# FFN rows turned by VectorE block transposes and DMAs instead of TensorE, with quotients on GpSimd and ScalarE and rounding in place

## The chip, the cores and the metric

The kernel runs on one core of a Trainium2 chip. The metric is the device time of one execution in microseconds (us); lower is better. A core has five engines that run side by side, each with an instruction stream of its own that is carried out in order: PE (TensorE, the matmuls, with PEld for its weight loads), DVE (VectorE), ACT (ScalarE), POOL (GpSimd) and SP (SyncE, which here issues DMAs). They wait for one another through semaphores.

## The reference

Sixteen sequences x of 256 rows and 256 channels pass through one block. Cut to what matters:

```python
# attention of 16 heads, projected, RMS-normalised, scaled and shifted by the condition
x1 = rwkv(adaln_attention(x))      # below
def rwkv(x):                       # x: (B, T, C); a shifted copy xx of x is mixed in
    k, v, r = xk @ Wk.T, xv @ Wv.T, xr @ Wr.T     # xk = x*mix_k + xx*(1-mix_k), and so on
    # scan over T: out_t = (a + exp(u + k_t) * v_t) / (b + exp(u + k_t))
    #              a, b = a*ew + exp(k_t)*v_t, b*ew + exp(k_t)
    return (sigmoid(r) * out) @ Wo.T
x = x + x1
x2 = quaternion_rotation(x)        # one 256 x 256 linear map
def fp4_linear(x, w):              # both operands rounded to FP4 in blocks of 16, with scales
    return einsum('bsk,nk->bsn', fp4_quant_dequant(x), fp4_quant_dequant(w))
gate, y = fp4_linear(x2, w_gate), fp4_linear(x2, w_up)         # 704 columns each
out = x + fp4_linear(silu(gate) * y, w_down)
```

## The kernel before, in words

Each of the 16 sequences (b from 0 to 15) goes through stages, each a Python generator that yields after a few instructions. The names in brackets are those of the stages in the order string.

- `ask` (a): load x, turn it (L599), project to q, k and v.
- `attend` (t): scores on PE (L650), exponentials on ACT (L659), values on PE (L671). `values` turns the sums into `u` on DVE (L681). `divide` then takes reciprocals (L688), multiplies (L690) and turns the rows back into `oT` (L696), all on DVE.
- `leave` (l): output projection, RMS norm and modulation, giving `xm` and the shifted `xx`.
- `mix` (m): the difference `d` on POOL (L759), three mixed inputs `mx` on DVE (L764), three projections on PE (L565), exponentials `ek` (L781) and `er` (L795) on ACT, two scans on DVE (L774). Then the quotient: `den` and `num` on DVE (L799, L803), `den` times 1 + er (L806), one reciprocal (L808), and the product `yT` on POOL (L811).
- `rotate` (r): output projection (the L565 with `wt_ao`), the residual `x1T` (L821), rotation (L826), a turn by 32 x 32 blocks (L830), rounding to FP4 (`quant`) and a turn back (L834).
- `hidden` (h for rows 0 to 127, i for rows 128 to 255): eight matmuls for gate and up (L847), tanh on ACT (L858), two products on DVE (L860, L864) and `quant` on the 704 columns.
- `quant`: block maxima, scale, reciprocal and a product on DVE (L486 to L490), absolute values on ACT (L492), two rounding steps on DVE (L494, L495), and the product with the scales on POOL (L498). It reads `src` and writes a tile `v` of its own.
- `turn_h` (d, e): the six 128-column pieces of a rounded row tile are transposed on PE (L541, by `turn_half`) and copied from PSUM to `hT` on ACT (L544, L549). `hT` has one buffer.
- `down` (f): twelve matmuls with `downT` and `hT` (L881), the sum with `x1T` and a turn on DVE (L886, L887), and four stores on SP (L892).

The weights go through similar stages at the start (W, V, with copies from PSUM on ACT at L533 and L544). Each matmul on f32 data shows as two records in the profile, each transpose as one.

The order of the instructions is not left to a scheduler. The string `ORDER` names one stage per word, and each word advances that stage by one yield; so it fixes the order on PE, ACT, DVE, POOL and SP:

```python
    with tc.manual_schedule(engines={E_.PE, E_.Activation, E_.DVE, E_.Pool, E_.SP}):
        for step in ORDER.split():
            if step not in made:
                made[step] = stages[step]()
            next(made[step])
```

The end of the string, from late in the last sequence's rotation, shows what runs there: `hf` and `if` are the two halves of its hidden stage, `fe` and `ff` the last two down projections.

```
rf fd he he he fd fd rf he if he ee if if he if if if if ee he he if ee hf if ee if if hf hf hf hf hf if if if
hf hf hf de hf de de hf de hf hf fe hf ef fe fe ef ef df ef fe fe df df df ff ff ff ff ff
```

After the main part a check of the reciprocals can branch to a slow exact path (`exact`, L923); with these inputs it is not taken.

Of the kernel before, what the change touches and what calls it, by code (L numbers as in the profile page):

```python
# [27 lines left out]
L L L L W1 L Q Q L a0 a0 W1 K L W1 W5 L K K Q Q W1 R L a0 W1 Q Q a0 a0 L a0 K R W5 K W5 R W1 a0 W1 A K a0 K t0 L  # L28
W0 A L W5 W5 t0 M A t0 W5 A R W5 a1 t0 M O t0 a1 t0 R W0 a1 W3 a2 W0 V0 t0 W3 O W2 t0 W3 W3 a1 t0 W0 R a1 t0 M
t0 R W0 a1 a1 t1 R A V0 W3 M a1 t1 t1 A W0 W3 t1 t0 W0 t1 V1 M R R t1 W3 t0 M W2 t1 a2 t0 t0 W2 A t0 t1 t1 a3 T  # L30
A t0 V0 V0 t0 V0 a2 t1 t1 W2 V1 a2 a2 a2 a3 W2 t1 t1 l0 t1 W4 t1 a2 T l0 V0 a2 t1 t1 t1 W4 l0 l0 l0 V0 a3 l0 t2
l0 m0 m0 V1 m0 t2 W4 W4 m0 W4 a3 a3 t2 m0 m0 a3 m0 m0 m0 t2 t2 t2 m0 l1 l1 m0 t2 m0 l1 l1 m0 m0 m0 m0 m0 t2 t2
l1 t2 V0 a3 t2 t2 a4 l1 l1 V0 t2 a3 r0 W2 W4 m1 m1 V1 r0 t2 t2 m1 m1 m1 V1 W2 m1 t3 m1 W4 t2 t2 r0 m1 t3 t2 r0
r0 a4 m1 t3 t3 t3 t3 r0 l2 l2 l2 m1 m1 m1 m1 m1 m1 m1 m1 l2 t3 t3 t3 r0 l2 a4 t3 l2 t3 t3 a4 a4 t3 l2 r1 r1 a4
a4 r0 r0 t3 r1 m2 t3 V1 V1 a5 a5 a4 m2 i0 t4 t3 r1 r1 t4 r1 m2 i0 i0 t3 t3 i0 i0 m2 m2 t4 i0 m2 m2 i0 i0 a6 i0
i0 i0 i0 i0 l3 l3 l3 l3 m2 m2 m2 m2 m2 t4 t4 t4 a5 a5 a5 a5 a5 t4 t5 r1 r1 m2 m2 m2 m2 h0 a5 h0 h0 t4 l3 r1 h0
t5 m2 i0 l3 h0 h0 h0 h0 h0 t5 l3 r2 t4 h0 h0 h0 t4 i1 i1 r2 h1 h1 h0 i1 i1 h1 t4 t4 i1 r2 r2 t4 h0 t4 h1 h1 t4
h1 h1 h1 r2 r2 a6 V1 t5 h1 t5 m3 t4 V1 h1 h1 r2 a6 a6 i1 t4 t4 r2 m3 i1 r2 h1 i1 i1 i1 i1 a7 a6 a6 t5 i1 h1 h1
m3 m3 i1 m3 m3 a6 a6 t5 t5 t5 t5 i2 i1 e0 t5 t5 i2 e0 t6 i2 i2 t6 t6 i2 m3 m3 m3 m3 i2 i2 i2 e0 t6 e0 i2 i2 i2
m3 m3 m3 d0 d0 t6 t6 h2 l4 m3 m3 m3 h2 l4 l4 h2 t5 m3 i2 h2 h2 h2 h2 l4 l4 t5 i2 h2 h2 h2 h2 i2 r3 t5 d0 r3 l4  # L40
t6 l4 t6 a7 t5 d0 h2 m4 m4 m4 m4 t5 a8 h2 t6 t6 m4 m4 a7 m4 t5 m4 r3 t6 m4 m4 t6 r3 a7 m4 t6 t6 m4 a7 m4 m4 m4
t6 a7 a7 l5 t7 r3 a7 m4 m4 t7 r3 r3 t6 l5 l5 r3 f0 t6 t7 l5 t6 t7 f0 f0 f0 t7 t7 d1 r4 r4 d1 d1 t7 d1 h2 l5 l5
l5 m5 a8 r4 t7 t7 f0 e1 r4 a8 r3 e1 r4 r4 m5 m5 i3 i3 i3 i3 a8 m5 t7 m5 i3 m5 m5 r4 r4 e1 e1 t7 t7 a8 a8 i3 i3
i3 i3 i3 i3 l6 t8 t8 t8 i3 i3 f1 t8 l6 l6 f1 h3 m5 t8 i3 l6 h3 m5 h3 h3 h3 l6 t8 l6 h3 h3 a8 a9 h3 t7 l6 t7 m5
m5 m5 h3 h3 h3 h3 a8 f1 m5 m5 m5 t8 m5 t8 m6 t7 t7 f1 m5 r4 t7 h3 t8 i4 i4 i4 i4 t8 t8 r5 r5 i4 i4 i4 e2 i4 a9
a9 e2 i4 m6 a9 i4 r5 i4 t8 r5 i4 t8 t8 t8 a9 a9 a9 e2 e2 t8 t7 h3 t9 r5 a9 r5 r5 t8 d2 d2 d2 d2 i4 l7 l7 m6 t9
m6 m6 l7 l7 i4 f2 m6 m6 m6 t9 h4 f2 m6 l7 h4 f1 h4 m6 t8 l7 h4 h4 l7 m6 m6 m6 m6 t9 m6 l8 m6 r5 l8 r5 h4 t9 l8
m6 l8 f2 f2 f2 h4 h4 i5 h4 h4 h4 i5 i5 i5 i5 r6 r6 l8 t9 h4 h4 l8 e3 t9 t9 e3 h4 aa aa l8 t9 i5 i5 aa t9 t9 m7
m7 i5 i5 d3 t9 t9 aa i5 d3 e3 i5 r6 r6 r6 e3 ab d3 d3 t9 m7 i5 i5 i5 aa aa aa h5 aa t9 h5 h5 h5 h5 h5 h5 h5 h5
h5 ta t9 m7 m7 r6 r6 m8 m7 h5 h5 m7 m8 f3 t9 f3 h5 ta f3 f3 ta f3 ta m7 r6 r6 ta h5 m8 ta d4 d4 e4 e4 m7 m7 m7  # L50
m7 m7 m7 m7 m7 m7 ta ta ta m8 m8 m8 ta i6 i6 i6 i6 i6 i6 i6 r7 m8 ta ta i6 i6 i6 h6 h6 r7 ab ta ac h6 m8 h6 h6
ta ta h6 i6 m8 m8 ab t9 h6 h6 h6 h6 ab ab ab i6 h6 ta i6 tb tb d4 ta h6 e4 m8 ta m8 h6 l9 d4 e4 ab r7 l9 i6 m8
f4 ab l9 m8 tb l9 h6 l9 m8 m8 m8 r7 f4 f4 r8 r7 e5 l9 l9 d5 tb r7 e5 d5 f4 r8 e5 m9 d5 m9 m9 m9 d5 m9 m9 la e5
r7 ac la r7 r7 la m9 m9 m9 la tb tb m9 m9 m9 m9 m9 m9 m9 m9 ac ac ac ac f5 f5 r8 r8 r8 la la la r8 r8 tb tb tb
r8 f5 f5 i7 i7 r8 ma tb tb tb i7 i7 i7 i7 i7 i7 i7 i7 i7 tc tc r9 r9 e6 h7 tc e6 i7 i7 ad ma ma ma tb tb h7 ad
h7 h7 tb r9 r9 f4 ac tc ac h7 r9 tc r9 i7 h7 h7 h7 h7 h7 tc h7 e6 e6 ma ma ma ma ma tb ma h7 tc tc tc tc ma ad
tb tb ma ma ma f5 h7 ad i8 i8 i8 i8 d6 i8 ad d6 h8 ad d6 d6 h7 ma ma h8 h8 h8 r9 ma h8 h8 h8 h8 i8 r9 h8 h8 h8
i8 i8 h8 r9 lb lb tc lb lb i8 i8 i8 f6 f6 f6 lb h8 h8 lb f6 e7 ra tc i8 e7 lb tc ra tc tc i8 f6 i9 i9 i9 i9 ra
mb mb i9 i9 i9 i9 ra i9 tc td ra d7 d7 ae tc ad i8 i9 i9 e7 td d7 tc ad mb mb ae d7 i9 e7 td mb mb h9 h9 h9 h9
td h9 h9 h9 af i9 ra lc ra ra td h9 h9 h9 h9 td lc lc lc td td i9 mb mb f7 mb mb h9 lc lc lc f7 f7 mb ra f7 mb  # L60
e8 ae mb ia td ia e8 mb ia ae mb h9 ia mc td mb mb ia ia ia ia ia f7 td ae ae d8 d8 ia ia ia h9 rb rb af mc ia
td td ae td td rb d8 d8 ae td te te ia mc mc ha rb rb td ha ha ha ha ha ha ha ha e8 mc ha ha td rb rb e8 te mc
mc mc te rb ha f8 mc mc mc mc ld te te mc ld rb mc ld f8 f8 mc mc mc te te te ld ib f8 ha d9 ib ib ib te te te
rc rc ib ib d9 ib ib ib ha f8 ld rc ld ld te te ib e9 hb af te e9 ib rc hb rc hb d9 ib hb rc te md md md af d9
hb e9 ib e9 ib te md md te C md rc af hb md af tf hb md hb f9 hb hb hb hb md md md md md md tf tf f9 f9 le le tf
tf f9 hb af rc rc ic ic le md f9 af le md md ic ic ic ic tf ic ic ic ic ic le rd le le ea tf rd ic me me da hb
ea ea ic ic rd da ea tf rd tf rd da me me me tf tf hc da me tf tf hc hc hc rd rd tf me hc me me me rd rd hc hc
tf hc hc hc hc hc tf tf tf fa fa me hc me me fa fa fa lf id lf id id me me lf lf eb eb C id lf id hc me lf lf db
id id id mf db hd id id id me hd db hd hd id hd re eb eb id re mf db hd hd fb hd hd hd hd fb dc re re id re hd
fb mf ec fb dc hd hd mf re ec ec mf mf re ec dc dc re mf mf mf mf fc ed re fc fc fc mf dd ed ie fc mf mf mf dd  # L70
mf mf mf ie ie ie ie ie ie ie ie ie ie ed ed fb rf ie C dd rf he he C ie dd ie he he rf rf rf fd rf he rf he fd
rf fd he he he fd fd rf he if he ee if if he if if if if ee he he if ee hf if ee if if hf hf hf hf hf if if if
hf hf hf de hf de de hf de hf hf fe hf ef fe fe ef ef df ef fe fe df df df ff ff ff ff ff
# [4 lines left out]
def kernel(  # L78
# [128 lines left out]
    def loads():  # L207
# [31 lines left out]
        load_w("av", a_v, "xr")  # L239
# [25 lines left out]
    gain = const.tile([P, E2, NB], F32, tag="gain", name="gain")  # L265
    uu = const.tile([P, E2], F32, tag="uu", name="uu")
# [42 lines left out]
    def turn_mask():  # L309
# [29 lines left out]
    def modulate():  # L339
# [5 lines left out]
        nc.vector.tensor_copy(wcT, pc[0:NC, :])  # L345
# [23 lines left out]
    def times():  # L369
        ew = const.tile([P, E2], F32, tag="ew", name="ew")  # L370
        nc.scalar.activation(ew, col("decay", 0, 2), AF.Exp, scale=1.0 / S)
        nc.scalar.activation(uu, col("first", 0, 2), AF.Exp, scale=1.0 / S)
        yield
        nc.vector.tensor_copy(ew_row, ew.unsqueeze(2).to_broadcast([P, E2, S]))
        yield
# [103 lines left out]
    def quant(src, n, tag, bufs, put=lambda dst: None):  # L479
        blk = lambda a: a.rearrange("p (b i) -> p b i", i=16)  # L480
        am = qp.tile([P, 44], F32, tag="am", name="am")[:, 0 : n // 16]
        rs = qp.tile([P, 44], F32, tag="rs", name="rs")[:, 0 : n // 16]
        v = qp.tile([P, 704], F32, tag="v", name="v")[:, 0:n]
        m = qp.tile([P, 704], BF16, tag="m", name="m")[:, 0:n]
        bc = lambda a: a.unsqueeze(2).to_broadcast([P, n // 16, 16])
        nc.vector.tensor_reduce(am, blk(src), AX.X, ALU.max, apply_absolute_value=True)  # L486
# [3 lines left out]
        nc.vector.scalar_tensor_tensor(blk(v), blk(src), -(1.0 - 2.0**-22), bc(rs), ALU.mult, ALU.mult)  # L490
# [17 lines left out]
    hT = wk.tile([P, FK, S], F32, tag="hT", name="hT")  # L508
    nc.gpsimd.memset(hT[FF % P : P, FK - 1, :], 0.0)
    nc.gpsimd.memset(downT[FF % P : P, FK - 1, :], 0.0)  # L510

    def in_weights(j):
        j *= 2 * P
        nt = min(2, (2 * FF - j) // P)
        n = nt * E
        raw = wk.tile([P, FF], F32, tag="h", name="raw", bufs=2)[:, 0:n]
        for jj in range(nt):
            lo, hi = j + jj * P, j + (jj + 1) * P
            for src, base in ((w_gate, 0), (w_up, FF)):
                a, b = max(lo, base), min(hi, base + FF)  # L520
                if a < b:
                    nc.sync.dma_start(out=raw[a - lo : b - lo, jj * E : (jj + 1) * E], in_=src[a - base : b - base, :])
        yield
        wq = yield from quant(raw, n, "hq", 4)
        pt = ps()
        for ct in range(E2):
            for jj in range(nt):
# [311 lines left out]
    def hidden(b, tt):  # L839
        xqT = xqs[b]  # L840
        for f in range(2):
# [20 lines left out]
            if f == 0:  # L862
                h = wk.tile([P, FF], F32, tag="h", name="h", bufs=2)
# [197 lines left out]
```

## Time and profile before

| | |
|---|---|
| median of 3 runs | 687.19 us (685.79 to 691.19) |
| profiled execution, its time | 686.15 us |
| its span, first to last instruction | 684.1 us |
| granted TensorE clock, mean | 0.994 |
| matmuls L847 (gate and up) | 512 records, 164.6 us busy |
| matmuls L881 (down) | 384 records, 90.2 us busy |
| transposes L541 | 204 records, 32.6 us busy (192 of hidden rows, 12 of weights) |
| copies into hT, ACT L544 and L549 | 15.2 + 12.0 + 8.4 us |
| product L498 with the scales, POOL, 704 columns | 1.40 us each, 34 of them |
| difference L759, POOL, 256 columns | 0.86 us each |

How to read it: "busy" is the time in which an engine has an instruction under way. A group's row gives line, engine, operation, what it writes and reads, shape and count, then busy time in us and the mean duration of one in ns, then the engine's idle time just before these instructions and what ended it. A PE record's duration includes the latency of the pipeline, so neighbouring matmuls overlap; their pace is the distance between their starts. A line of the timeline gives the start, the time from the first start to the last end of the merged instructions, and their number.

### The profile page before, as it was taken

How to read it: one execution, taken by the hardware profiler on the slowest of the kernel's cores; microseconds unless marked ns; L12 is line 12 of the kernel's file. 1: busy time of each engine (PE TensorE's matmuls, PEld its weight loads, DVE VectorE, ACT ScalarE, POOL GpSimd, SP SyncE). 2: the span in 40 equal slices, each digit the busy share in tenths (PEclk: the TensorE clock that was granted, in tenths of full speed). 3: DMA queues.
4: the chain of work that ended last, by engine and by line, in shares of the span. 5: the costliest groups of instructions: out<-in, count | busy, mean ns of one | idle time of the engine just before them, and what ended most of it. 6: DMA issues, size and time to landing. Idle time of an engine off the chain costs nothing. (4 is left out here: it accounts for less than half of the span.)

```text
span 684.1 us, 10332 instructions
## 1 busy us (share of the span) xinstructions
PE 661.7 (97%) x3880; PEld 464.2 (68%) x3880; DVE 587.8 (86%) x991; ACT 349.1 (51%) x765; POOL 142.7 (21%) x171
## 2 busy tenths in 40 slices
PE   7999999999999999999999999999999999898994
PEld 6657667656676666766667866767767676676663
DVE  6788797899996787888989888998899999999981
ACT  2777774655645645565435554455544556332230
POOL 4712220311203110122103110222112213111210
PEclk9999999999999999999999999999999999999997
DMA  6410000000001000020000100010000000001001
GB/s 173 116 53 17 1 16 17 1 16 0 1 17 32 1 3 15 0 47 1 16 17 0 32 16 2 0 32 1 17 0 17 1 16 1 16 1 31 13 4 36
DMA packets 39726, 13.61 MB, mean 20 GB/s; under 512 B 36068, under 2 KB 39284, under 8 KB 39668
## 3 DMA queue, kind: packets, MB, share of 16 engines
q1 hardware_dynamic: 39552, 12.85, 7.6%
q8 instruction: 32, 0.52, 0.3%
q14 instruction: 26, 0.21, 0.1%
q10 hardware_dynamic: 116, 0.02, 0.0%
HBM read 8.67 MB, written 4.19 MB: 19 GB/s over the span
## 5 line engine op out<-in xcount | busy, mean ns | idle before, releaser
L847 PE MATMUL ps<-guT,xqT 128*128 128x352 f32 x512 | 164.6, 463 | 0.7 <-DVE xqT L834 0.4
L659 ACT ACTIVATE w<-pss 128x512 f32<-128x512 f32 x256 | 135.2, 606 | 52.0 <-PE pss L650 51.6
L847 PEld LDWEIGHTS ps<-guT,xqT 128*128 128x128 f32 x512 | 94.4, 190 | 57.0 <-issue 5.0
L498 POOL TENSOR_TENSOR hq<-v,am 128x704 f32<-128x704 f32 (+2 forms) x40 | 54.0, 1350 | 190.0 <-DVE v L495 116.9
L881 PE MATMUL ps<-hT,downT 128*128 128x256 f32 x384 | 90.2, 387 | 1.3 <-DVE xr L830 0.7
L881 PEld LDWEIGHTS ps<-hT,downT 128*128 128x128 f32 x384 | 73.2, 193 | 16.1 <-issue 2.3
L492 ACT ACTIVATE m<-v 128x704 bf16<-128x704 f32 (+2 forms) x56 | 40.6, 727 | 67.7 <-DVE v L490 58.4
L650 PE MATMUL pss<-qT,kT 32*128 32x512 f32 x512 | 73.7, 640 | 0.0
L858 ACT ACTIVATE th<-ps 128x352 f32<-128x352 f32 x64 | 30.0, 468 | 62.3 <-PE ps L847 57.0
L671 PE MATMUL ps<-w,v_one 128*32 128x256 f32 x1024 | 61.3, 382 | 0.0
L494 DVE SCALAR_TENSOR_TENSOR v<-m,v 128x704 f32<-128x704 bf16 (+2 forms) x56 | 48.1, 859 | 7.7 <-ACT m L492 7.6
L808 DVE RECIPROCAL den<-den 128x512 f32<-128x512 f32 x16 | 53.6, 3351 | 0.4
L671 PEld LDWEIGHTS ps<-w,v_one 128*32 128x32 f32 x1024 | 30.3, 109 | 28.0 <-issue 4.4
L495 DVE SCALAR_TENSOR_TENSOR v<-m,v 128x704 f32<-128x704 bf16 (+2 forms) x56 | 45.7, 816 | 1.9
L544 ACT COPY hT<-ps 128x384 f32<-128x384 f32 (+1 forms) x64 | 26.8, 428 | 34.9 <-PE ps L541 29.8
L860 DVE SCALAR_TENSOR_TENSOR th<-th,ps 128x352 f32<-128x352 f32 x64 | 32.1, 502 | 11.6 <-ACT th L858 11.5
L811 POOL TENSOR_TENSOR yT<-num,den 128x512 f32<-128x512 f32 x16 | 20.4, 1274 | 93.3 <-DVE den L808 89.0
L864 DVE SCALAR_TENSOR_TENSOR h<-th,ps 128x352 f32<-128x352 f32 x64 | 33.0, 515 | 6.2 <-PE ps L847 2.3
L541 PE MATMUL ps<-ident,hq 128*128 128x128 f32 (+1 forms) x204 | 32.6, 277 | 5.0 <-POOLq L1011 2.8
L541 PEld LDWEIGHTS ps<-ident,hq 128*128 128x128 f32 (+1 forms) x204 | 23.6, 136 | 20.3 <-issue 5.7
L650 PEld LDWEIGHTS pss<-qT,kT 32*128 32x128 f32 x512 | 20.5, 182 | 23.2 <-issue 19.6
L498 POOL TENSOR_TENSOR xq<-v,am 128x512 f32<-128x512 f32 x16 | 18.4, 1148 | 78.1 <-DVE v L495 78.1
(164 smaller groups left out, 1140.9 us busy)
## 6 DMA issues: line engine op xcount, KB each, us to landing
x_sb<-in_x_dram SPq DMA_DIRECT2D x64, 64.0 KB, 2.1
out_dram<-o_sb SPq DMA_DIRECT2D x64, 64.0 KB, 1.8
raw<-in_L_ffn_w_down_dram SPq DMA_DIRECT2D x2, 352.0 KB, 3.0
raw<-in_L_ffn_w_gate_dram SPq DMA_DIRECT2D x5, 128.0 KB
raw<-in_L_ffn_w_up_dram SPq DMA_DIRECT2D x5, 128.0 KB
ek<-in_L_cond_Wq_dram SPq DMA_DIRECT2D x1, 256.0 KB, 2.9
er<-in_L_cond_Wk_dram SPq DMA_DIRECT2D x1, 256.0 KB
kv<-in_L_cond_Wv_dram SPq DMA_DIRECT2D x1, 256.0 KB, 3.2
```

What stands on the lines that cost most here:

```text
L492: nc.scalar.activation(m, v, AF.Abs, scale=2.0**22)
L494: nc.vector.scalar_tensor_tensor(v, m, 1.5 * 2.0**22, v, ALU.max, ALU.add)
L495: nc.vector.scalar_tensor_tensor(v, m, 1.5 * 2.0**22, v, ALU.max, ALU.subtract)
L498: nc.gpsimd.tensor_tensor(blk(dst), blk(v), bc(am), ALU.mult)
L541: nc.tensor.transpose(pt[0:n, (k - k0) * P : (k - k0 + 1) * P], src[:, k * P : k * P + n], ident)
L650: nc.tensor.matmul(quad[r], kT[rows_, g, kt * P : (kt + 1) * P], qT[rows_, g].rearrange("p i q -> p (i q)"), start=True, stop=True,)
L659: nc.scalar.activation(w[:, kt, r].rearrange("p i q -> p (i q)"), quad[r], AF.Exp)
L671: nc.tensor.matmul(pu[32 * r : 32 * r + 32, i * S : (i + 1) * S], vo[:, kt, 8 * g + 2 * r + i, :], w[:, kt, r, i, :], start=(kt == 0), sto ...
L808: nc.vector.reciprocal(flat(den), flat(den))
L847: nc.tensor.matmul(p_[:, 0:FH], xqT[:, ct, tt * P : (tt + 1) * P], guT[:, ct, base + f * FH : base + (f + 1) * FH], start=(ct == 0), stop= ...
L864: nc.vector.scalar_tensor_tensor(h[:, fs], th, 0.5, pair[1], ALU.mult, ALU.mult)
L881: nc.tensor.matmul(pdn[:, 0:S], downT[:, k, h * P : (h + 1) * P], hT[:, k, :], start=(k == 0), stop=(k == FK - 1))
```

## The change

1. Hidden rows. `turn_h` no longer uses PE and ACT. DVE turns each 128 x 704 tile in blocks of 32 x 32 into `hturned`, and a new stage `move_h` (g) issues 16 DMAs per sequence that carry the blocks between partition groups into `hT`. SP issues them; for the last sequence ACT issues half. The columns of `guT` are permuted so that these moves are of 640 or 768 consecutive bytes, and `hT` is laid out as 8 groups of 32 columns per k, so L881 (L963 after) reads it in runs of 32.
2. Quotients. The mixed inputs `mx` become a product on ACT and a sum on POOL, as do `den` and `num`. The reciprocal L808 becomes a starting value by exponential on the bits (ACT), one cubic and one Newton step, with five POOL products (one of them takes in `num`), a minimum on POOL and four ACT instructions. The last product writes `yT`. `er`, `kv` and `ek` serve as scratch and stay in use until then.
3. `divide` multiplies on POOL instead of DVE and yields between its three instructions; `on` has two buffers.
4. Rounding in place: `quant` writes over its input. `h`, `raw`, `xr`, the mask and the rounded values share one set of four buffers; `hq` has two buffers, not four, and `res` one, not two.
5. In the weight stages the copies to `guT` and `downT` go to DVE, three other small copies to ACT.
6. `ORDER` is new throughout. Its end:

```
if if if if hf hf if if if de if hf if hf hf hf hf hf if ge hf hf ge if hf ef fe hf hf hf fe df gf fe gf fe
ff ff ff ff ff
```

```diff
-    def quant(src, n, tag, bufs, put=lambda dst: None):
+    def rounded(n):
+        return qp.tile([P, 704], F32, tag="v", name="v", bufs=VB)[:, 0:n]
+
+    def quant(v, n, tag, bufs, put=lambda dst: None):
...
-        v = qp.tile([P, 704], F32, tag="v", name="v")[:, 0:n]
...
-        nc.vector.scalar_tensor_tensor(blk(v), blk(src), -(1.0 - 2.0**-22), bc(rs), ALU.mult, ALU.mult)
+        nc.vector.scalar_tensor_tensor(blk(v), blk(v), -(1.0 - 2.0**-22), bc(rs), ALU.mult, ALU.mult)
...
-    hT = wk.tile([P, FK, S], F32, tag="hT", name="hT")
+    hT = wk.tile([P, S // 32, FK, 32], F32, tag="hT", name="hT")
+    R_AT, R_N = (0, 192, 384, 544), (192, 192, 160, 160)
...
             nc.vector.reciprocal(rec, u[:, :, :, D])
-            on = att_p.tile([P, S // 32, 2, D], F32, tag="on", name="on")
-            nc.vector.tensor_tensor(
+            yield
+            on = att_p.tile([P, S // 32, 2, D], F32, tag="on", name="on", bufs=2)
+            nc.gpsimd.tensor_tensor(
...
             mx[nm] = wk.tile([P, S], F32, tag="mx" + nm, name="mx")
-            nc.vector.scalar_tensor_tensor(mx[nm], d, col("mix_" + nm), xx, ALU.mult, ALU.add)
+            nc.scalar.activation(mx[nm], d, AF.Identity, scale=col("mix_" + nm))
+            yield
+            nc.gpsimd.tensor_add(mx[nm], mx[nm], xx)
...
         for t in range(E2):
-            nc.vector.scalar_tensor_tensor(den[:, t, :], ek[:, t, :], uu[:, t : t + 1], sb[:, t, :], ALU.mult, ALU.add)
+            nc.scalar.activation(den[:, t, :], ek[:, t, :], AF.Identity, scale=uu[:, t : t + 1])
+        yield
+        nc.gpsimd.tensor_add(flat(den), flat(den), flat(sb))
...
         nc.vector.scalar_tensor_tensor(flat(den), flat(er), 1.0, flat(den), ALU.add, ALU.mult)
         yield
-        nc.vector.reciprocal(flat(den), flat(den))
-        yield
+        nc.gpsimd.tensor_scalar(flat(den), flat(den), 2.0**125, None, ALU.min)
+        yield
+        r_, t_, s_ = flat(er), flat(kv), flat(ek)
+        nc.scalar.activation(r_, flat(den).bitcast(I32), AF.Exp, bias=lift, scale=-LN2 / 2.0**23)
+        yield
+        nc.gpsimd.tensor_tensor(t_, flat(den), r_, ALU.mult)
+        yield
+        nc.scalar.activation(s_, t_, AF.Square, bias=low15)
+        nc.scalar.activation(s_, s_, AF.Identity, bias=c75)
+        yield
+        nc.gpsimd.tensor_tensor(r_, r_, s_, ALU.mult)
+        nc.gpsimd.tensor_tensor(t_, flat(den), r_, ALU.mult)
+        yield
+        nc.scalar.activation(s_, t_, AF.Identity, bias=two, scale=-1.0)
+        yield
+        nc.gpsimd.tensor_tensor(r_, r_, flat(num), ALU.mult)
         yT = wk.tile([P, E2, S], F32, tag="yT", name="yT", bufs=2)
-        nc.gpsimd.tensor_tensor(flat(yT), flat(num), flat(den), ALU.mult)
+        nc.gpsimd.tensor_tensor(flat(yT), r_, s_, ALU.mult)
...
     def turn_h(b, tt):
-        hq = hqs.pop((b, tt))
-        for k0 in range(0, FK, 3):
-            yield from turn_half(hq, hT[:, :, tt * P : (tt + 1) * P], k0)
+        if b not in turned:
+            turned[b] = wk.tile([P, T2, FF], F32, tag="hturned", name="hturned")
+        nc.vector.transpose(turned[b][:, tt], hqs.pop((b, tt)))
+        yield
+
+    def move_h(b):
+        t = turned.pop(b)
+
+        def move(engine, q):
+            for r in range(4):
+                engine.dma_start(
+                    out=hT[32 * r : 32 * r + 32].rearrange("p (t q) k i -> p t q (k i)", t=T2)[:, :, q, 0 : R_N[r]],
+                    in_=t[32 * q : 32 * q + 32, :, R_AT[r] : R_AT[r] + R_N[r]],
+                )
+
+        for q in range(4 if b < B - 1 else 2):
+            move(nc.sync, q)
+        yield
+        if b == B - 1:
+            for q in range(2, 4):
+                move(nc.scalar, q)
+        yield
...
-                    pdn[:, 0:S], downT[:, k, h * P : (h + 1) * P], hT[:, k, :], start=(k == 0), stop=(k == FK - 1)
+                    pdn[:, 0:S], downT[:, k, h * P : (h + 1) * P], hT[:, :, k, :], start=(k == 0), stop=(k == FK - 1)
...
-            res = io.tile([P, S], F32, tag="res", name="res", bufs=2)
+            res = io.tile([P, S], F32, tag="res", name="res", bufs=1)
```

Line numbers after the change, where the prediction uses them: L513 and L514 are L494 and L495 before, L814 is the scan L774, L850 is L806, L934 the new block transpose, L942 the new DMAs, L963 is L881.

## The prediction

> **What bounds the kernel now.** I read the page's busy times first, then the table of stretches, which says where the bound changes.
>
> ```profile
> PE 661.7 (97%) x3880; PEld 464.2 (68%) x3880; DVE 587.8 (86%) x991; ACT 349.1 (51%) x765; POOL 142.7 (21%) x171
> ```
>
> ```profile
> core 0: us, PE busy (x) PEld busy (x) DVE busy (x) ACT busy (x) POOL busy (x), PEclk, DMA share, GB/s
> 0.00:40.00 40.00, 34.28 (x199) 24.51 (x199) 28.16 (x63) 22.15 (x44) 22.38 (x55) 1.00 0.48 132
> 40.00:600.00 560.00, 557.35 (x3381) 387.27 (x3381) 493.85 (x817) 307.43 (x674) 106.96 (x106) 1.00 0.05 12
> 600.00:628.60 28.60, 28.20 (x131) 22.05 (x130) 27.53 (x48) 8.21 (x20) 5.53 (x4) 1.00 0.01 3
> 628.60:666.90 38.30, 33.87 (x143) 24.08 (x141) 35.04 (x59) 10.46 (x25) 6.49 (x5) 1.00 0.08 19
> 666.90:684.10 17.20, 7.96 (x30) 6.27 (x30) 3.21 (x8) 0.90 (x3) 1.39 (x1) 0.78 0.15 36
> ```
>
> From 40 to 600 PE is busy 557 of 560 us at the full granted clock, with DVE at 88%: work taken off PE there is time. From 628.6 (the last batch's L806) to 666.9 DVE is busy 35.0 of 38.3 us and PE stands idle 4.4: the tail is DVE's. The last 17.2 us are a chain: last product on POOL, turn, L881, result, store.
>
> The paces come from the timeline:
>
> ```profile
> 649.49 0.49 PE L541 MATMUL ps<-ident,hq 128*128 128x128 f32 x3
> 649.82 3.72 PE L847 MATMUL ps<-guT,xqT 128*128 128x352 f32 x12
> 653.37 0.49 PE L541 MATMUL ps<-ident,hq 128*128 128x128 f32 x3
> 653.70 4.90 PE L847 MATMUL ps<-guT,xqT 128*128 128x352 f32 x16
> ...
> 668.43 0.88 PE L541 MATMUL ps<-ident,hq 128*128 128x128 f32 x6 [2.83 <-POOLq L1011]
> ```
>
> Three transposes start at 649.49 and the next matmul 0.33 later: 0.109 each, though one shows 0.277. In the same way L847 goes at 0.296 a record, and a record of 256 columns at 0.215.
>
> The work that changes engine (by form):
>
> ```profile
> L808 DVE RECIPROCAL den<-den 128x512 f32<-128x512 f32 x16 | 53.6, 3351 | 0.4
> L764 DVE SCALAR_TENSOR_TENSOR mx<-d,cols,xx_lo 128x256 f32<-128x256 f32 x48 | 29.6, 643 | 2.4 <-POOL d L759 1.4 <-PE ps L565 1.0
> L690 DVE TENSOR_TENSOR on<-u,recs 128x256 f32<-128x256 f32 x32 | 20.3, 636 | 1.1
> ...
> L811 POOL TENSOR_TENSOR yT<-num,den 128x512 f32<-128x512 f32 x16 | 20.4, 1274 | 93.3 <-DVE den L808 89.0 <-PE ps L565 4.3
> ```
>
> The means of L764 and L690 are too long for 256 columns (L764's median is 477). The timeline shows why, on a scan:
>
> ```profile
> 577.88 2.08 DVE L774 TENSOR_TENSOR_SCAN bs<-ew_row,ek 128x255 f32<-128x255 f32 x2
> 578.04 1.37 POOL L498 TENSOR_TENSOR xq<-v,am 128x512 f32<-128x512 f32 x1 [5.51 <-DVE v L495]
> ...
> 581.00 1.27 DVE L774 TENSOR_TENSOR_SCAN as<-ew_row,kv 128x255 f32<-128x255 f32 x2
> ```
>
> Two scans that take 1.27 alone take 2.08 with a POOL product beside them: a DVE instruction with two SBUF operands waits out a running POOL product. Such stretches sum to about 27 us here.
>
> Last, what a DMA costs its queue (the stores), and its landing (the x loads):
>
> ```profile
> L892 SPq DMA_DIRECT2D out_dram<-o_sb x64: 315/460/557, 214.4 to 679.0; - x64
> ```
>
> ```profile
> DMA to landing us min/median/max: 2.0/2.1/3.4
> ```
>
> **The change part by part.**
> PE: 192 transposes of hq go: 192 x 0.109 = 20.9 us. The upper end is their share of the group's busy time, 32.6 x 192/204 = 30.7. I take 20.9 and 2 more for the small waits around them.
> ACT loses L544 and L549 into hT (15.2 + 12.0 + 8.4) and some weight copies (4.6) and gains 112 products of 256 columns at about 0.47 (L729) and 64 of 512 at 0.60 (L781), 91 us: 349 becomes 400, 60%.
> DVE loses L808 (53.6), L764, L690, L799, L803 (78.3) and gains 32 block transposes of 704 columns (0.446 at 256 and 0.698 at 512 give 0.87 each, 28 us) and some 7 us of weight copies: 588 becomes about 490.
> POOL gains 96 products of 512 at 1.27 (122 us), 80 of 256 at 0.73 to 0.86 (L759, 63 us), and 16 minima between 0.52 (a memset of 512) and 1.27, taken as 0.9 (14 us): 143 becomes about 340, half the span.
> SP gains 16 DMAs a batch: 16 x 0.5 = 8 us of issue, then 2.1 to land, 10 us from turned rows to hT. Stores and x loads queue behind up to 8 us; x is loaded a batch ahead, so that hides.
>
> Middle. In the built order the last L565 of the last batch (its ar projection) has 591.8 us of PE work before it now, 569.3 after, at the paces above: 22.5 less. It ends at 625.7 now, so 603.2. Then:
> - transposes' waits: -2.
> - DVE has more slack (88% to about 75%): -3, between 0 and -12. PE's work ends 33.9 us behind its paces now, 8.4 of it idle in the first two stretches, so 25 in small waits; -12 is half of them.
> - The port. Port-taking DVE instructions fall to about 17 a batch, 272; now some 416 lose 27 us, 0.064 each, beside POOL at 16.5% tensor work; at 47% that scales to 0.18 each, about 50 us, so DVE is near 515 without the old 27, still not the bound. For late pieces that PE then waits for: +3, between 0 and 12.
> - hT has one buffer: between two down projections must lie 10 us. The order leaves 5.2, 9.7 and 9.5 us of PE work between some late ones: +4, between 0 and 6.
> - The strided read of hT by L881 has no like row: the nearest, L437 on tiles read by every second column, starts 0.118 apart against 0.109. 0 to +7 (8% of 384 x 0.215); I take 0, as runs of 32 stay together.
> - Rounding in place adds and removes no instruction; h, raw, xr and v share four buffers where h and v had two each. A block waits at most for one POOL product (1.4) to free one, and PE's work beside it covers that: 0, at worst +1.4 at each of a few places. In the head the small copies that swap ACT and DVE weigh some 3 us on either, with both at 70% or less there: 0, up to 3 either way.
> The quotient chain after er grows from 6.2 us (0.6 + 0.69 + 3.35 + 1.27, hops) to about 11.3 on three engines, but the order puts 12.9 to 32.7 us of PE work in it for the batches before the last: 0.
> Sum 605.2.
>
> Tail. From L806 to the last L495 DVE has 35.7 us of instructions now and takes 38.2. In the new order, from L850 to the last turn, it has 42.2: no reciprocal, but six turns (5.2) and three more result pairs (2.6) fall here. After ar 3.0 as now, L850 0.7, 42.2, gaps 1.8, wait for the last POOL product 0.6: 653.5. The last move is split over SP and ACT: 8 x 0.5 + 2.0 = 6.0, where six transposes and a copy take 1.2 now. L881 7.1, end 7.4 as now (676.7 to 684.1): span 674.0. The profiled execution took 686.15 for a span of 684.1, and 686.15 is 1.0 below the median: 674.0 + 2.05 + 1.0 = 677.
>
> So some 23 us come off PE, and the tail gives about half back.
>
> The Trainium skill, "SBUF — State Buffer", section "Who interferes with whom", says that the port pair between VectorE and GpSimd is an exclusive lock and the loser blocks for the whole instruction. The scan above agrees (0.81 lost). If every one of 272 instructions met a full 1.27 us product, that rule would make an estimated 345 us of waits and a slower kernel; no run here shows so dense a meeting.
>
> **The rivals.**
> B, the tail hides its additions. PE is full to the end: 684.1 - 30.7 + about 2 for the hop = 655.4, 658. For it: the order was rebuilt, so the last batch may start earlier against the rest. Against it: DVE's 42.2 us of rows.
> C, the chains on three engines are late. If each of the six POOL products in a quotient chain waits out a DVE instruction (0.89), it takes 16.6; the batches with 12.9, 14.1, 13.6 and 14.5 us of cover then stall PE 3.7, 2.5, 3.0 and 2.1, 11 us in all: 688.
> D, slower: DVE becomes the bound through the port. By rows it has 506 us, 461 of it ahead of L850's last. It may be stretched there by 72 us (0.88 x 606 - 461) before it is as loaded as now; beyond that each us counts. Slower than 694 needs some 17 more: 90 us over 272 instructions, 0.33 each. Against it: 0.18 scaled. For it: with POOL's products back to back a scan loses the port again at each handoff, as in the scan above; random meeting with half-run products gives 0.47 x 0.64 = 0.30. At 0.36 each: 698.
> E, the hop or the strided read costs its upper end (+2 and +7): 686.
>
> **How the numbers follow.** Forecast 0.45, B 0.12, C and E 0.23, D 0.20. Own range of the forecast 668 to 684. The range for 8 in 10 takes in B's and D's points: 658 to 698. A measurement here can tell about 1% from no change, that is 680.3 to 694.1. Faster: B and most of the forecast, 0.55; same: the forecast's upper part and C and E, 0.25; slower: D, 0.20.
>
> **What would show it.** PE busy near 635 and no hq transposes. DVE near 510, POOL near 340, ACT near 400. From L850 of the last batch to the last turn about 45 us, from there to the first L963 matmul of that batch about 6. Scans and L513 stretched, 40 to 60 us in all. Wrong if PE has gaps of over 20 us between 40 and 590 (C or D: then DVE is at 90% or waits on POOL), if the tail after L850 takes less than 55 us to the last matmul (B), or if the down matmuls go slower than 0.215 (E).

## The result, and the profile after

The changed kernel takes 712.86 us (median of 4 runs, 712.65 to 713.35) against 687.57 for the kernel before (4 runs, 685.79 to 691.19): a ratio of 1.036, 95% interval 1.032 to 1.041. It is slower; 677 was predicted, between 658 and 698. The profiled execution took 712.65 us for a span of 710.9, against 686.15 and 684.1.

The engines' loads first, from the page of after:

```profile
PE 656.5 (92%) x3688; PEld 453.0 (64%) x3688; DVE 534.7 (75%) x888; ACT 400.9 (56%) x837; POOL 357.1 (50%) x367
```

Work moved as the diff says: 192 records fewer on PE, DVE 53 us lighter, POOL 214 heavier. PE's busy time fell by only 5 us while its share fell from 97% to 92%. The table of stretches of after, cut where the prediction cuts (the last sequence's L850 begins at 627.4 and its last block turn ends at 686.7), shows where:

```profile
core 0: us, PE busy (x) PEld busy (x) DVE busy (x) ACT busy (x) POOL busy (x), PEclk, DMA share, GB/s
0.00:40.00 40.00, 34.37 (x203) 24.87 (x203) 30.67 (x73) 21.04 (x44) 22.38 (x60) 1.00 0.55 145
40.00:600.00 560.00, 549.63 (x3233) 374.21 (x3232) 435.88 (x703) 360.69 (x758) 305.96 (x285) 0.99 0.11 25
600.00:627.40 27.40, 20.78 (x81) 15.79 (x80) 23.00 (x38) 9.25 (x18) 11.84 (x11) 0.94 0.21 49
627.40:686.70 59.30, 42.62 (x146) 31.19 (x147) 42.52 (x71) 9.94 (x17) 16.96 (x13) 0.86 0.18 42
686.70:710.90 24.20, 9.14 (x29) 6.91 (x27) 2.63 (x7) 0.00 (x0) 0.00 (x0) 0.72 0.24 56
```

Two things changed. From 600 on PE is idle for 38 us (7.7 of them behind the last matmul) and the granted clock falls to 0.94, 0.86 and 0.72. And from 40 to 600, with DVE at 78% where it had 88%, PE got no further: it did 3233 records against 3381, and 138 of the 148 that are missing are the transposes of hidden rows that the diff takes away.

Busy time hides part of this, because a matmul that starts late still counts as busy. So I count PE's work at its paces (0.296 us for a record of 352 columns, 0.215 for 256, 0.109 for a transpose, and in the same way from the distance of starts 0.135 for a score and 0.054 for a value record) and call the time beyond that "behind". The third column is the experiment that turns the rows on PE again.

| us | before | after | after, rows turned on PE |
|---|---|---|---|
| PE's work at its paces | 632.9 | 612.0 | 632.9 |
| behind, up to 600 | 32.5 | 48.5 | 43.1 |
| behind, from 600 to the end | 18.7 | 50.4 | 27.5 |
| span | 684.1 | 710.9 | 703.5 |

The 20.9 us that the diff takes off PE are there. Against them PE loses 16.0 more up to 600 and 31.7 more after it, 47.7 in all, so the span grows by 26.8.

The tail of after, from its timeline (start, time, engine and instructions merged, in brackets the idle time before and what ended it):

```profile
611.33 4.51 PE L963 MATMUL ps<-hT,downT 128*128 128x256 f32 x12 [3.07 <-DMA hT<-hturned]
616.54 2.75 PE L963 MATMUL ps<-hT,downT 128*128 128x256 f32 x12
630.87 5.28 PE L963 MATMUL ps<-hT,downT 128*128 128x256 f32 x12 [6.39 <-DMA hT<-hturned]
653.29 4.32 PE L963 MATMUL ps<-hT,downT 128*128 128x256 f32 x12 [3.65 <-DMA hT<-hturned]
680.76 6.83 PE L963 MATMUL ps<-hT,downT 128*128 128x256 f32 x24 [8.73 <-DMA hT<-hturned]
694.97 8.25 PE L963 MATMUL ps<-hT,downT 128*128 128x256 f32 x24 [7.37 <-DMA out_dram<-o_sb]
...
641.75 10.18 SPq L942 DMA_DIRECT2D hT<-hturned  x16
668.79 23.96 SPq L942 DMA_DIRECT2D hT<-hturned  x24
680.72 0.91 DVE L934 STREAM_TRANSPOSE hturned<-hq 128x704 f32<-128x704 f32 x1 [3.24 <-DMA hT<-hturned]
687.63 5.57 ACTq L942 DMA_DIRECT2D hT<-hturned  x8
```

The kernel before, in the last two sequences:

```profile
662.52 2.76 PE L881 MATMUL ps<-hT,downT 128*128 128x256 f32 x12
...
669.61 7.08 PE L881 MATMUL ps<-hT,downT 128*128 128x256 f32 x24 [0.30 <-ACT hT L544]
```

In after, each of the last five down projections waits for its move, 29.2 us in all. (The last wait is put down to a store; it needs the 16 moves of that sequence as well, of which ACT issues its eight up to 693.2, two us earlier.) Sixteen moves occupy SP for 10.2 us, 0.64 each. And the twelve matmuls that follow a wait take 4.3 to 5.3 us where the next twelve take 2.75: the granted clock is 0.5 from 611.9 for 3.4 us, from 629.0 for 6.8, from 652.9 for 3.4, from 676.8 for 6.8 and from 690.5 for 10.2.

DVE is caught in the same waits. Its waits in the stretch from 627.4 to 686.7 of after (waited for: us in total, times, longest):

```profile
DVE res L968 <- PE ps L963: 10.0, 4, 5.5
DVE hturned L934 <- DMA hT<-hturned: 3.2, 1, 3.2
```

DVE carries out its stream in order, so `res` waiting for a late L963 holds up the rows of the last sequence queued behind it; and `hturned`, one buffer, is not free until the move before has read it.

### The profile page after: what moved, and what is told of

Read it like the earlier page. It is cut to its first block, busy times and chain, and to the rows that moved or that the text cites. A ratio compares the mean times of both kernels' runs of the same rounds, so it can differ in the third digit from the quotient of the medians.

```text
span 710.9 us, 10524 instructions
## 1 busy us (share of the span) xinstructions
PE 656.5 (92%) x3688; PEld 453.0 (64%) x3688; DVE 534.7 (75%) x888; ACT 400.9 (56%) x837; POOL 357.1 (50%) x367
## 4 chain that ended last, share of the span: by engine, by line
PE 64%; DVE 11%; SPq 10%; DMA 4%; POOL 4%; issue 3%; ACT 2%; ACTq 0%; DVEq 0%; POOLq 0%
PE ps L601 19%; PE ps L907 13%; PE ps L963 11%; SPq L942 9%; PE pss L686 7%; PE ps L707 6%; PE ps L613 5%; DMA hT<-hturned 2%; PE ps L886 1%; DVE v L509 1%; DVE am L505 1%; DVE v L514 1%; POOL den L854 1%; DVE v L924 1%; DVE den L850 1%
## 5 line engine op out<-in xcount | busy, mean ns | idle before, releaser
L963 PE MATMUL ps<-hT,downT 128*128 128x256 f32 x384 | 98.5, 413 | 31.2 <-DMA hT<-hturned 23.3
L963 PEld LDWEIGHTS ps<-hT,downT 128*128 128x128 f32 x384 | 78.7, 208 | 52.7 <-issue 34.0
L513 DVE SCALAR_TENSOR_TENSOR v<-m,v 128x704 f32<-128x704 bf16 (+2 forms) x56 | 53.8, 961 | 8.9 <-ACT m L511 8.8
L514 DVE SCALAR_TENSOR_TENSOR v<-m,v 128x704 f32<-128x704 bf16 (+2 forms) x56 | 58.0, 1036 | 1.9
L509 DVE SCALAR_TENSOR_TENSOR v<-v,rs 128x704 f32<-128x704 f32 (+2 forms) x56 | 52.5, 938 | 1.9
L804 POOL TENSOR_TENSOR mx<-mx,xx_lo 128x256 f32<-128x256 f32 x48 | 38.0, 806 | 31.4 <-ACT mx L802 31.3
L841 POOL TENSOR_TENSOR den<-den,bs 128x512 f32<-128x512 f32 x16 | 21.4, 1336 | 63.8 <-ACT den L839 61.3
L727 POOL TENSOR_TENSOR on<-u,recs 128x256 f32<-128x256 f32 x32 | 22.6, 705 | 56.7 <-DVE recs L724 56.7
L505 DVE TENSOR_REDUCE am<-v 128x44 f32<-128x704 f32 (+2 forms) x56 | 44.4, 794 | 1.7 <-DMA v<-in_L_ffn_w_gate_dram 0.4
L934 DVE STREAM_TRANSPOSE hturned<-hq 128x704 f32<-128x704 f32 x32 | 28.4, 891 | 18.5 <-DMA hT<-hturned 18.4
L686 PEld LDWEIGHTS pss<-qT,kT 32*128 32x128 f32 x512 | 21.7, 182 | 26.8 <-issue 18.7
L924 DVE SCALAR_TENSOR_TENSOR v<-th,ps 128x352 f32<-128x352 f32 x64 | 32.9, 514 | 7.1 <-PE ps L907 2.8
```

The source lines that it names most:

```text
L505: nc.vector.tensor_reduce(am, blk(v), AX.X, ALU.max, apply_absolute_value=True)
L509: nc.vector.scalar_tensor_tensor(blk(v), blk(v), -(1.0 - 2.0**-22), bc(rs), ALU.mult, ALU.mult)
L513: nc.vector.scalar_tensor_tensor(v, m, 1.5 * 2.0**22, v, ALU.max, ALU.add)
L514: nc.vector.scalar_tensor_tensor(v, m, 1.5 * 2.0**22, v, ALU.max, ALU.subtract)
L686: nc.tensor.matmul(quad[r], kT[rows_, g, kt * P : (kt + 1) * P], qT[rows_, g].rearrange("p i q -> p (i q)"), start=True, stop=True,)
L963: nc.tensor.matmul(pdn[:, 0:S], downT[:, k, h * P : (h + 1) * P], hT[:, :, k, :], start=(k == 0), stop=(k == FK - 1))
```

## The experiments

All but those called "the kernel before with ..." start from the changed kernel. The kernel before measured 687 to 688 us beside each group. Times are medians; ratios are against the kernel before.

**1. The moves on two queues.** SP and ACT issue eight each for every sequence.

```diff
-        for q in range(4 if b < B - 1 else 2):
+        for q in range(2):
             move(nc.sync, q)
+            move(nc.scalar, q + 2)
         yield
-        if b == B - 1:
-            for q in range(2, 4):
-                move(nc.scalar, q)
```

> Every move is split over two queues, eight DMAs on SP and eight on ACT, for all sequences instead of the last alone. Theory H (the hop bounds the late part: 16 issues at 0.64 us and 1.9 us of landing, one hT and one hturned, PE idle until it lands, then half the clock): a hop falls from about 12.2 to about 7.5 us, the waits of PE before L963 (3.1, 6.4, 3.7, 8.7 us for the sequences 11 to 14) shrink by about 4 each, some drops of the clock go: 690 to 700 us. Theory P (GpSimd's load, its port and the long quotient chain make DVE and PE late everywhere): no gain, 708 to 716, as ACT is held up by eight more issues a sequence.

743.56 us, 1.079 (1.074 to 1.083). Both theories missed it. ACT's waits in this kernel:

```profile
ACT w L695 <- DMA hT<-hturned: 22.6, 4, 8.3
ACT mx L802 <- DMA hT<-hturned: 16.7, 3, 6.6
```

The issues themselves, in the same kernel (number, nanoseconds of one as minimum, median and maximum, first and last start), and ACT's waits for a semaphore ahead of them:

```profile
L942 SPq DMA_DIRECT2D hT<-hturned x128: 585/595/1049, 171.9 to 723.9; - x128
L942 ACTq DMA_DIRECT2D hT<-hturned x128: 592/607/862, 178.7 to 724.3; - x128
L942 ACTq EVENT_SEMAPHORE  x46: 17/17/7061, 220.1 to 724.2; - x46
```

An issue keeps its engine for 0.6 us, on ACT as on SP. The 128 issues take 80 us of ACT, eight in a row 5.2 to 8.3 us, and ACT's other work (exponentials `w`, products `mx`) stands behind them in the stream. Of the 71 us of ACT's waits that are put down to these DMAs, 58 are issues under way and only 0.4 are semaphore waits ahead of an issue (the one long wait, 7.06 us, comes at 711.4). So it is mostly the issuing that holds ACT, not a wait for `hT`. On SP the same issues hold up only other DMAs. Theory P named this hold, but 31 us were far from its "no gain". This run says nothing on how long the hop is.

**2. No refinement of the quotient.** It leaves out the cubic and the Newton step: four POOL products and three ACT instructions a sequence.

```diff
-        nc.gpsimd.tensor_tensor(t_, flat(den), r_, ALU.mult)
...
-        nc.gpsimd.tensor_tensor(flat(yT), r_, s_, ALU.mult)
+        nc.gpsimd.tensor_tensor(flat(yT), r_, flat(num), ALU.mult)
```

> Leaves out the cubic and the Newton step: yT is the starting value of the reciprocal times num. Four POOL products and three ACT instructions fewer a sequence, about 85 us less on POOL, and about 9 us off the quotient chain. The steps stay in the order, empty. Theory P: DVE's stretches fall by a third, PE's small waits from 100 to 600 us fall by 8 or more, the last quotient comes 9 us earlier: 690 to 700. Theory H: the hops stay as they are, 706 to 712.

708.94 us, 1.029 (1.025 to 1.033). This is in theory H's range. The chain's refinement is worth 4 us. POOL's busy time fell from 357 to 264 us, and the waits for the moves in the tail stayed as they were.

**3. Rows turned on PE again.** Transposes and ACT copies in the d and e steps, two `hT` buffers, no moves.

```diff
-        nc.vector.transpose(turned[b][:, tt], hqs.pop((b, tt)))
+        for k0 in range(0, FK, 3):
...
+                nc.tensor.transpose(pt[0:n, (k - k0) * P : (k - k0 + 1) * P], hq[:, k * P : k * P + n], ident)
...
+            nc.scalar.copy(dst[:, k0 : k0 + full, :], pt[:, 0 : full * P].rearrange("p (k t) -> p k t", t=P))
```

> Undoes the hop alone: the hidden rows are transposed on PE again and copied to hT by ACT, in the step in which DVE turned them, with two hT buffers in place of hturned; guT in its old column order; the quotients, divide, rounding in place and the rest of the order as after the change. PE gets 20.9 us of work back. Theory H: PE's waits for hT (23 us for the DMAs and 7 for the last ones) and the half clock after them (about 10) go, so 712 + 21 - 30 - 10, 688 to 698. Theory P: the work on PE is simply added where DVE and POOL are late, 708 or more.

705.96 us, 1.025 (1.021 to 1.030): between the two. The move costs 5.4 us of lateness up to 600 and 22.9 after it (third column of the table), against 20.9 of PE work saved: 7 us net. (The run takes back the move and its single `hT` together; how much each costs is not shown.) Nineteen us remain that are not the move. In the last two down projections of this kernel no move is waited for, and the matmuls go at full clock:

```profile
682.03 0.88 PE L933 MATMUL ps<-ident,hq 128*128 128x128 f32 x6 [2.62 <-POOL hq L517]
682.74 5.35 PE L952 MATMUL ps<-hT,downT 128*128 128x256 f32 x24
...
689.47 5.45 PE L952 MATMUL ps<-hT,downT 128*128 128x256 f32 x24 [0.24 <-ACT hT L935]
```

**4. PE kept warm.** 28, 56, 32, 76 and 64 transposes of the identity ahead of the down projections of sequences 11 to 15, in PE's idle time.

```diff
+            if h == 0:
+                for _ in range({11: 28, 12: 56, 13: 32, 14: 76, 15: 64}.get(b, 0)):
+                    nc.tensor.transpose(pdn[:, 0:P], ident, ident)
```

> Adds idle work to PE: 28, 56, 32, 76 and 64 transposes of the identity, overwritten afterwards, ahead of the down projections of sequences 11 to 15, where PE otherwise waits for hT. If the half clock comes from PE's idleness and lies on the path, the twelve to twenty-four matmuls that follow run at 0.215 us a record again (2.75 us for twelve, not 4.5 and 5.3) and the time falls by 5 to 11: 701 to 707. If they are slow because hT is read in runs of 32 or written by DMAs beside it, they stay slow: 711 to 716.

703.19 us, 1.022 (1.017 to 1.026), 9.7 less than after. The last two down projections in its timeline:

```profile
674.76 5.42 PE L966 MATMUL ps<-hT,downT 128*128 128x256 f32 x24 [0.45 <-DMA hT<-hturned]
687.44 5.42 PE L966 MATMUL ps<-hT,downT 128*128 128x256 f32 x24 [0.27 <-issue]
```

5.42 where after had 6.83 and 8.25, and the granted clock stays at 1.0 from 82 to 696. Useless work made the kernel faster: the half clock after a wait lay on the path.

**5 and 6. What is left without the quotient's part.** Number 5 puts mx, den, num and the quotient back on DVE (the move stays); number 6 does so with the rows turned on PE, the product of `divide` on DVE and two `res`, so that only the new order, rounding in place and the weight copies are left of the change.

```diff
-            nc.scalar.activation(mx[nm], d, AF.Identity, scale=col("mix_" + nm))
             yield
-            nc.gpsimd.tensor_add(mx[nm], mx[nm], xx)
+            nc.vector.scalar_tensor_tensor(mx[nm], d, col("mix_" + nm), xx, ALU.mult, ALU.add)
...
-        nc.gpsimd.tensor_scalar(flat(den), flat(den), 2.0**125, None, ALU.min)
+        nc.vector.reciprocal(flat(den), flat(den))
```

> After, with the quotient and the mixed inputs back on VectorE (mx, den and num in one instruction each, one reciprocal, one product on POOL); the new order, the move of the hidden rows by DMA, the product of divide on POOL and rounding in place stay. Undoing the move by DMA alone left 706. Theory T, the rest is the work that went from DVE to POOL and ACT (longer chains, port): 690 to 700, as about 7 us of the move remain. Theory O, the rest is the new order and the shared buffers: 706 to 714.

> After, with the transposes on PE, the quotient, the mixed inputs and the product of divide on VectorE, two hT and two res buffers again: of the change only the new order, rounding in place with shared buffers and the weight copies on DVE are left. Theory T: 684 to 692, about as before. Theory O: 700 to 707 or later, as when the move by DMA alone was undone, since DVE has its 588 us back as well.

742.07 us, 1.076 (1.070 to 1.081), and 724.60, 1.050 (1.045 to 1.054). Theory T, that the moved work is what costs, said 690 to 700 and 684 to 692: it falls in this form. Theory O missed number 5 too (706 to 714); only its "or later" for number 6 holds. PE's waits in number 5:

```profile
PE ps L895 <- DVE th L908: 13.0, 6, 3.4
PE ps L601 <- DVE mx L803: 10.1, 6, 4.0
```

The new order was laid out for a lighter DVE; with the old load in it PE waits for DVE. So the new order can't be judged with the old work in it, and the next runs go the other way, into the old order.

**7. The kernel before with rounding in place.** One set of four buffers, one `res`.

```diff
-        v = qp.tile([P, 704], F32, tag="v", name="v")[:, 0:n]
...
-                h = wk.tile([P, FF], F32, tag="h", name="h", bufs=2)
+                h = rounded(FF)
```

> The kernel before in its own order, with nothing but rounding in place: h, raw, xr, the mask and the rounded values in one set of four buffers, one res buffer; hq keeps four. If the shared buffers cost what is left: 695 to 706. If they cost nothing (theory T, or theory O by the order alone): 685 to 690.

686.90 us, 0.997 (0.994 to 0.999). In before's order the shared buffers cost nothing.

**8. The kernel before with a warm tail.** `warm` is 26 for the first turn of the last sequence and 0 elsewhere.

```diff
+        for _ in range(warm):
+            nc.tensor.transpose(pt[:, 0:P], ident, ident)
```

> The kernel before, with 26 dummy transposes of the identity on PE ahead of the last sequence's first turn, where PE stood idle 2.83 us and the granted clock then fell to a half during the last down projection. If the half clock there lies on the path: the last 24 matmuls go from 7.1 to about 5.3 us and the time to 685 to 686. If not: 687, or later by what the dummies delay.

685.94 us, 0.9973 (0.9947 to 0.9999): at most half a per cent, hardly more than the measurement can tell. In its trace the last 24 matmuls take 5.45 us at the full clock, where before had 7.08:

```profile
670.12 5.45 PE L883 MATMUL ps<-hT,downT 128*128 128x256 f32 x24 [0.29 <-ACT hT L546]
```

**9 and 10. The kernel before with the sums moved.** Number 9 moves mx, den and num to ACT and POOL; number 10 puts the coarse starting value in place of the reciprocal as well. Both keep before's order, with the added words beside the old.

```diff
-            nc.vector.scalar_tensor_tensor(den[:, t, :], ek[:, t, :], uu[:, t : t + 1], sb[:, t, :], ALU.mult, ALU.add)
+            nc.scalar.activation(den[:, t, :], ek[:, t, :], AF.Identity, scale=uu[:, t : t + 1])
+        yield
+        nc.gpsimd.tensor_add(flat(den), flat(den), flat(sb))
```

> The kernel before in its own order, with one part of the change: mx, den and num as a product on ACT and a sum on POOL (the POOL sums follow the ACT products by two words of the order), the reciprocal stays on DVE. DVE loses 78 us and gains no turns. If the new order is what costs the rest (706 with PE turns), this is no slower than before: 680 to 688. If the moved sums themselves cost it (POOL's port, later mx and den): 692 to 705.

> As the kernel before with mx, den and num on ACT and POOL, and the reciprocal replaced by a minimum on POOL and the starting value by exponential on ACT; it leaves out the cubic and the Newton step, so the quotient is a coarse one. DVE loses 132 us in all. The chain after er is about as long as before's (0.9 + 0.6 + 1.3 and hops against 3.35 + 1.27). If the new order is what costs the rest: 676 to 688. If the moved work itself costs it: 695 to 710.

713.82 us, 1.035 (1.032 to 1.038), and 706.98, 1.026 (1.021 to 1.032). Neither kernel gains from the lighter DVE (556 us busy in number 9, 505 in number 10, against 588): the moved work itself costs time in the old order, in number 9 more than the 705 foreseen.

**11. PE turns in the tail alone.** Sequences 0 to 10 keep the move; 11 to 15 are turned on PE, in pieces of 32 columns (the columns of `guT` stay permuted), into `hT` and the room of `hturned` by turns.

```diff
+                        nc.tensor.matmul(
+                            pt[32 * r : 32 * r + 32, (k - k0) * P : (k - k0 + 1) * P], hq[:, at : at + 32], ident,
+                            start=True, stop=True,
+                        )
```

> After, with the move by DMA for sequences 0 to 10 only; the rows of sequences 11 to 15 are turned on PE again (by products with the identity in pieces of 32 columns) into hT and, every other sequence, into the room of hturned. If the move pays where PE has other work (14 of the 21 us it saves, at some 5 us of waits) and loses only in the tail (23 us later there than with PE turns): 694 to 702, less than either after or the kernel with all rows on PE (706). If the move costs as much in the middle: 705 or more.

698.89 us, 1.013 (1.011 to 1.016), in the range for a move that pays only with cover: 14 less than after, 7 less than with all rows on PE. Its last four groups of down matmuls, in the timeline:

```profile
652.24 2.75 PE L982 MATMUL ps<-hT,downT 128*128 128x256 f32 x12
658.85 2.75 PE L982 MATMUL ps<-hT,downT 128*128 128x256 f32 x12
677.02 5.45 PE L982 MATMUL ps<-hturned,downT 128*128 128x256 f32 x24
683.86 5.45 PE L982 MATMUL ps<-hT,downT 128*128 128x256 f32 x24
```

No wait before them and no half clock in them.

**12 to 14. Port or handoff, den or mx.** In before's order: number 12 (with rounding in place) adds the same POOL sums, which nothing reads, and leaves DVE its work; 13 moves mx alone; 14 moves den and num alone.

```diff
+            idle = wk.tile([P, 2 * S], F32, tag="idle", name="idle")
+            nc.gpsimd.tensor_add(idle[:, 0:S], d, xx)
```

> The kernel before with rounding in place (687 by itself) and its own order; added are 48 sums of 256 and 32 sums of 512 columns on POOL at the same places of the order as the moved sums, written to a tile that nothing reads; DVE keeps all of its work. Theory port (POOL's sums hold up VectorE's instructions wherever they meet): 698 to 712, as DVE is even fuller here than with the sums moved (714). Theory handoff (the sums cost because other engines must wait for them): 686 to 692.

> The kernel before in its own order with mx alone as a product on ACT and a sum on POOL. Theory handoff by den (VectorE stood 45.7 us in the den times 1 + er instruction waiting for POOL's sum, when mx, den and num were all moved: 714): 686 to 694. If mx carries the loss, by projections that start late: 700 to 712.

> The kernel before in its own order with den and num alone as products on ACT and sums on POOL. Theory handoff by den: 700 to 712, with DVE again waiting 40 us or more in its den instruction. If mx carries the loss: 686 to 694.

694.17 us, 1.009 (1.006 to 1.012); 683.90, 0.993 (0.991 to 0.996); 714.63, 1.037 (1.033 to 1.041). Number 12 falls between its two theories: POOL's hold on DVE costs 7 us here (against 687 for rounding in place alone). mx costs nothing, and may gain 0.7%. den and num lose 26 by themselves, more than POOL's hold explains. DVE's and then PE's waits in number 14 (the profile is of its slowest run, 721.48):

```profile
DVE den L811 <- POOL den L802: 47.4, 13, 6.2
```

```profile
PE ps L852 <- DVE xqT L839: 5.2, 3, 4.1
PE ps L566 <- POOL yT L816: 4.9, 2, 3.5
PE ps L852 <- DVE u L682: 3.6, 3, 1.7
```

The sum of `den` is read by DVE's next instruction, so DVE stands until ACT and POOL are through, and what is queued behind (`xqT`, `u`) reaches PE late; the PE waits shown are a part of the 26 us. mx is read by PE, which has other work.

**15. The same handoffs in the new order.** From the changed kernel, den and num alone back on DVE, and the product of `divide` alone back on DVE.

```diff
-            nc.gpsimd.tensor_tensor(
+            nc.vector.tensor_tensor(
                 on.rearrange("p q i d -> p i q d"),
```

> After, with den and num back on VectorE in one instruction each, at the words of the POOL sums; all else as after. Theory handoff (VectorE waits 11.2 us in the den times 1 + er instruction for POOL's sum, and what is queued behind it is late): 703 to 710. Theory load (the new order was laid out for a VectorE without these 28 us, and any work put back makes PE's producers late): 714 to 725.

> After, with the product of divide back on VectorE at the same word; all else as after. Theory handoff (VectorE waits 15.7 us in the turn into oT for POOL's product): 703 to 711. Theory load: 714 to 722.

714.35 us, 1.037 (1.034 to 1.041), and 711.12, 1.032 (1.028 to 1.036), after being at 712.86. The first is at the lower edge of theory load, the second at the upper edge of theory handoff, and neither matters: in the order laid out for them these handoffs seem to cost about what the DVE time is worth.

**16. Versions to beat both.** mx alone (number 13) has the lowest median of all, 683.90, about 0.7% below before. Rounding in place and the warm tail together gave 686.68 (0.997, interval 0.9945 to 0.9996). All three:

> A version to beat both: the kernel before with mx moved to ACT and POOL (0.9934 by itself), rounding in place and the 26 dummy transposes in the tail. If the parts add: 0.987 to 0.991, some 680 to 682. If only mx counts: 0.993.

685.87 us, 0.997 (0.995 to 0.999). The parts don't add, and the gain of mx alone isn't seen again here (rounding in place alone had 686.90).

## Why the prediction was wrong, step by step

- **"192 x 0.109 = 20.9"**: right, 632.9 to 612.0. The 2 us more for the small waits around the transposes aren't to be seen.
- **Loads**: ACT 400 (400.9) and POOL 340 (357.1) were close; DVE near 515 was 534.7. The stretches of DVE beside POOL, each instruction's excess over the quarter-point of its kind where it is over 0.06 us, sum to 45 us (40 to 60 foretold, 27 before), all of them beside a running POOL instruction. As a time the port got +3, between 0 and 12; number 12 shows 7 for such sums in the old order. The Trainium skill's rule on the exclusive lock ("SBUF — State Buffer", "Who interferes with whom") is borne out by these stretches, but they are a side cost. Rival D, VectorE as the bound, did not come: DVE is at 78% from 40 to 600. (Its sum has a slip: by its own rule of 72 us free, 0.36 us on each of 272 instructions gives 703 and not 698. The range would still have ended below 712.9.)
- **"SP gains 16 DMAs ... 16 x 0.5 = 8 us"**: 0.64 each, 10.2 us, and 1.9 to land: a hop of 12 us, not 10.
- **Middle, "hT has one buffer ... +4, between 0 and 6"**: 5.4, right for the part up to 600.
- **Middle, "DVE has more slack ... -3" and the quotient chain at 0**: failed. The kernel with rows on PE is 10.6 us further behind at 600 than before. DVE's slack was worth nothing. That the work which left DVE came back as waits between engines is shown in the old order (9, 10, 14) and only argued for the new one. The refinement costs 4 us over the whole run (2); rival C had 11 for its chains. The sign set for C and D, PE gaps of over 20 us, did not come (10.4 us idle from 40 to 600), because this lateness hides in PE's busy time.
- **Strided read of `hT`, 0**: right. Twelve L963 take 2.75 at full clock, twelve L881 took 2.76.
- Between 600 and 624.5 come another 5 us: the first wait for a move (3.07) and the slow clock after it (4.51 for 2.75). So the last projection of the mix stage ended at 624.5, not at 605.2.
- **Tail, "42.2, gaps 1.8"**: the step that failed most. DVE's instructions there were 42.5 us, but it waited 16.8 in 59.3. I treated the last sequence as a chain on DVE alone and charged the single `hT` only in the middle. In the tail the moves lie in that chain: DVE's `res` waits 10.0 for down projections that wait for a move, and 3.2 for `hturned`.
- **"The last move ... 6.0"** took 8.2 from the last turn to the first matmul; **"L881 7.1"** took 8.25, mostly at half clock. Half the clock after a wait stood in no term of its own, though the 7.1, read off before, held 1.6 of it (number 8). Number 4 puts it at 9.7 us in after.
- **The range** took the rivals one at a time. The middle (about 19 late) and the tail (about 18) missed in the same direction, with the move in both.

Shown by runs: the net 7 us of the move with its single `hT`, its gain among the first eleven sequences and its loss in the tail (3, 11), the clock's 9.7, a part of that loss (4), the refinement's 4 (2), that rounding in place is free in the old order (7). Open: how the other 19 us of number 3 divide. A loss of that size also comes without the new order: number 10, in the old one and without the refinement, takes 707.0 where number 3 takes 706.0. In the old order den and num carry the loss (14), in the new one putting them back changes nothing (15) and putting everything back is worse (5, 6). An order laid out anew for mx moved and den and num on DVE was not tried. In the old order that mix gives 683.9 (13); in the new one, with the moves and the refined quotient as well, 714.4 (15). The moves with a second `hT` weren't tried either.

## What to carry to other kernels

Work taken off an engine that is not the bound was worth nothing by itself here; look at who reads the result next. In the order of the kernel before, a sum whose reader has other work (mx, read by PE) could go to another engine at no cost, and sums of which one is read by the next instruction of an in-order engine (den) could not. A longer way through DMAs may replace PE work where more PE work covers it, but keep the short way for the last sequences, where nothing does, and count the slow clock after each wait with it.

## What the runs showed of the hardware

- In after, from 100 us on, each of PE's six waits of 2.3 to 8.7 us goes with 3.4 to 10.2 us at a granted clock of 0.5. The half clock begins 2.5 to 4.8 us after PE's last work, and in the three longest waits (6.4 to 8.7 us) before the wait is over. The shortest of the six, in the timeline of after:

```profile
502.53 3.63 PE L601 MATMUL ps<-yT,wt_ao 128*128 128x256 f32 x8 [2.34 <-DVE v L924]
...
643.42 1.89 PE L601 MATMUL ps<-yT,wt_ao 128*128 128x256 f32 x8
```

The same eight records take twice as long after a wait of 2.34 us; the clock is at 0.5 from 502.7 to 506.1. The length of one wait alone doesn't decide it. After the first of the following lines (after) the clock is at 0.5 from 79.5 for 3.4 us; after the second (number 11), and after the wait of 2.62 us at 682.0 in number 3, it stays at 1.0:

```profile
77.88 1.61 PE L686 MATMUL pss<-qT,kT 32*128 32x512 f32 x4 [1.02 <-ACT w L695]
```

```profile
675.59 1.50 PE L946 MATMUL ps<-ident,hq 128*32 128x128 f32 x44 [2.86 <-POOL hq L517]
```

The Trainium skill, "TensorE: Matmul & The Clock Gate", section "HAM oscillation — how this bites in real kernels", warns of idle gaps above some 3.4 us; here 2.34 was enough.
- A DMA issue occupies the engine that makes it: in number 1 the median is 0.607 us on ACT and 0.595 on SP, over 128 each. With the gaps between them, 16 on SP take 10.18 us in after, and eight on ACT 5.57.
